# Four cross-attention layers on one core: the maximum's quarters and spread in the maximum's own PSUM banks, and grouped logits issued between the masked exponentials with their maxima held back

## The chip, the core and the metric

One NeuronCore of one Trainium2 chip runs the whole program. The metric is the device time of the core in microseconds; lower is better. Three runs of the kernel before gave 3663.92, 3665.89 and 3667.55 us, a median of 3665.89 us.

## What is computed

Four attention layers, one after the other, on four batch entries of 512 positions by 256 channels, all in 32-bit floats. Layers 0, 2 and 3 are "masked": 16 heads of 64, keys and values from a context of 1024 positions by 512 channels, with a bias of -20 on a few context positions where a mask over query positions is 0. Layer 1 is "grouped": an RMS norm, 16 query heads of 16 and 4 key and value heads.

```python
# layers 0, 2, 3 (T = 1024 keys, HW = 512 queries, HEAD_DIM = 64)
q = hidden_states @ Wq
k = encoder_hidden_states @ Wk
v = encoder_hidden_states @ Wv
...
logits = jnp.einsum('bhqd,bhkd->bhqk', q, k) * scale
logits = logits + col_bias[None, None, :, :]
probs = jax.nn.softmax(logits, axis=-1)
out = jnp.einsum('bhqk,bhkd->bhqd', probs, v)
out = out.transpose(0, 2, 1, 3).reshape(B, HW, HEADS * HEAD_DIM)
out = out @ Wo + bo
out = out + residual
# layer 1
xn = rmsnorm(x, norm_w)
...
scores = jnp.einsum('btgrd,bsgd->bgrts', qg, k) * scale
attn = jax.nn.softmax(scores.astype(jnp.float32), axis=-1).astype(q.dtype)
out = jnp.einsum('bgrts,bsgd->btgrd', attn, v).reshape(B, T, N_HEADS * HEAD_DIM)
return residual + out @ wo
```

## The kernel before

**Units and steps.** A unit is two heads of one layer of one batch entry: 96 masked units (three layers, four entries, eight units) and 32 grouped ones. Two strings, `MASKED_TURNS` and `GROUPED_TURNS`, give 96 steps; each step has one masked unit `g`, and 32 of them, from the 13th to the 74th, also have a grouped unit `lam`. Within a batch entry the grouped units come in every second step, and the last two in neighbouring steps. At the step before its own, a grouped unit is called `coming`: there its logits are made. The masked unit of the step before is `g1`.

**Tiles.** A unit's logits are held transposed, keys on partitions: eight tiles `g.st[t]` of 128 x 1024 (128 keys, two heads of 512 queries). TensorE makes a tile in two PSUM banks, ScalarE copies it to SBUF, and VectorE keeps a running maximum over the tiles in the two banks of tile 0, `g.mx_place`. `max_quarters` (line 759) reduces this maximum over partitions: a reduction with 32 x 32 transposes into one bank (L755), then small copies and maxima (L765 to L770). `max_everywhere` (line 775) spreads the result over all partitions with a transpose (L781), for a masked unit into two further banks, for a grouped one into SBUF. Then the tiles are lowered by it (L789 on VectorE for masked, L787 on GpSimd for grouped units) and ScalarE takes the exponential in place (L795). GpSimd adds a masked unit's exponentials up (L834). `attend` (L734) multiplies by the values one step later for a masked unit, and in the same step for `lam`. `normalise` (VectorE, L755 to L880) turns the sums into reciprocals, through one scratch bank, and scales the output; `project_out` (L898) adds it to the state.

**PSUM.** There are eight banks. The class `Place` gives out one bank, or an even-odd pair, when an instruction is issued; `back` returns it and numbers the return. A pair is the one whose later return is oldest; a single bank is the one with the oldest return, where 2 is added if the other half of its pair is free too. The place is a matter of issue order only: on the chip, the next user of a bank waits until the last one has read it.

**The order.** Every engine runs its instructions in the order in which the program issues them; that order is written out by hand. A step issues, in turn: for `lam`, the eight subtractions on GpSimd; the scores of `g` (L704, L710; copies L714, maxima L718); a single bank for the output of `g1` (`place_out`); the first four exponentials of `lam`; the maximum of `g`; `attend(g1)`. Then comes a list `fill` of TensorE work with estimated durations: the output projections, the query projections (L622, copy L628), and in odd steps the keys of the next two masked units (four halves of two parts, L526, copy L531), in even steps their values (L565, copy L572). Keys, values and queries each take a single bank, which is returned when the copy is issued. A clock `now` adds up the estimates. Three kinds of work are put in by due time:

- the subtractions and exponentials of `g` and the rest of `lam`'s exponentials are `events`; `pass_events(now)` issues those that are due just before the copy of a fill item;
- `pairs`: each of four pairs of logits tiles of `coming` (`logits_pair`, L681, copies L687, maxima L693), from 13.0 in steps of 2.5 (12.0 if there is a `lam`). Before the first pair, `behind_exponentials` issues all events that are left, and what was put off in `late`: `normalise(g1)` and the end of `lam`'s output. After the fourth pair come `max_quarters` and `max_everywhere` for `coming`;
- `attend_grouped`, the attention of `lam`, is put into `fill` once 9.5 of work stand before it (and after all projections of grouped outputs).

DMA loads for later steps are issued at the end of a step on SyncE.

Of the kernel before, what the change touches and what calls it, by code (L numbers as in the profile page):

```python
# [12 lines left out]
ALU = mybir.AluOpType  # L13
# [7 lines left out]
NT = T // P  # L21
# [61 lines left out]
def kernel(ctx: ExitStack, tc: tile.TileContext, a: dict, out: bass.AP):  # L83
    nc = tc.nc
# [8 lines left out]
    def t_(shape, tag, name, bufs=1, dtype=FP):  # L93
        return sb.tile(shape, dtype, tag=tag, name=name, bufs=bufs)
# [4 lines left out]
    ps_all = ps.tile([P, 8, S], FP, tag="ps", name="ps")  # L99
    given_back = dict.fromkeys(range(8), 0)  # L100
    returns = [0]

    class Place:
        def __init__(self, width=2):
            free = given_back
            if width == 2:
                at = min(
                    (n for n in range(0, 8, 2) if n in free and n + 1 in free),
                    key=lambda n: max(free[n], free[n + 1]),
                )  # L110
            else:
                at = min(free, key=lambda n: free[n] + (2 if n ^ 1 in free else 0))
            self.banks = range(at, at + width)
            for n in self.banks:
                del free[n]
            self.ap = ps_all[:, at : at + width, :].rearrange("p n q -> p (n q)")
# [13 lines left out]
    def take_set(g):  # L130
        g.set = sets_free.pop(sets_free.index(min(sets_free)))
        g.st = [st_slot((NT + 1) * g.set + t) for t in range(NT)]
        g.mx = st_slot((NT + 1) * g.set + NT)

    def give_set(g):
        sets_free.append(g.set)
# [539 lines left out]
    def logits_pair(g, i):  # L676
        ws = [Place(), Place()]
        for odd in range(2):
            for j in range(2):
                rows = slice(64 * odd + 32 * j, 64 * odd + 32 * (j + 1))  # L680
                nc.tensor.matmul(  # L681
                    ws[odd].ap[:, j * S : (j + 1) * S], lhsT=g.kt[rows, i * P : (i + 1) * P],
                    rhs=g.qt[rows, :], start=True, stop=True,
                )
        for odd, w in enumerate(ws):
            t = 2 * i + odd
            nc.scalar.copy(g.st[t], w.ap)  # L687
            if t == 0:
                g.mx_place = w
            else:  # L690
                w.back()
                top = g.mx_place.ap
                nc.vector.tensor_tensor(top, top, g.st[t], ALU.max)  # L693

    def scores(g):
        take_set(g)
# [23 lines left out]
    def place_out(g, width=1):  # L720
        g.place = Place(width)
        g.po, g.psum = g.place.ap[:, 0:S], g.place.ap[:, S:]

    def attend(g, blocks=range(NT)):
        for t in blocks:
            for j in range(2):
                rows = g.rows[j]
                if not g.masked:
                    rows = slice(64 * g.h + 32 * j, 64 * g.h + 32 * (j + 1))
                at, first, last = rows, 0, NT - 1  # L730
                if not g.masked:
                    at = slice(64 * (t % 2) + 32 * j, 64 * (t % 2) + 32 * (j + 1))
                    first, last = t % 2, NT - 2 + t % 2
                nc.tensor.matmul(  # L734
                    g.po[at, :], lhsT=g.v[:, t, rows], rhs=g.st[t][:, j * S : (j + 1) * S],
                    start=(t == first), stop=(t == last),
                )

    def keep_even(g):


        if g.h == 0:
            gq[g.b, "o"] = t_([P, S], "o1", f"o1_{g.name}")
        nc.scalar.copy(gq[g.b, "o"][64 * g.h : 64 * (g.h + 1), :], g.po[0:64, :])

    def keep_odd(g):
        half = gq[g.b, "o"][64 * g.h : 64 * (g.h + 1), :]
        nc.vector.tensor_tensor(half, half, g.po[64:128, :], ALU.add)  # L748
        g.place.back()
# [4 lines left out]
    def over_quarter(out_, of, op):  # L754
        nc.vector.tensor_reduce(  # L755
            out_, of.rearrange("p (b x) -> p b x", x=32), AX.X, op, apply_transpose=True
        )

    def max_quarters(g):
        w = Place(1)  # L760
        quarter, half = w.ap[:, 0:32], w.ap[0:64, 32:64]
        other = t_([64, 32], "other_max", f"other_max_{g.name}")
        over_quarter(quarter, g.mx_place.ap, ALU.max)
        g.mx_place.back()
        nc.vector.tensor_copy(other, quarter[64:128, :])  # L765
        nc.vector.tensor_tensor(half, quarter[0:64, :], other, ALU.max)
        nc.vector.tensor_copy(other[0:32, :], half[32:64, :])
        g.every = t_([P, 2 * S // 32, 1], "every", f"every_{g.name}")
        for h in range(4):
            nc.vector.tensor_tensor(  # L770
                g.every[32 * h : 32 * (h + 1), :, 0], half[0:32, :], other[0:32, :], ALU.max
            )
        w.back()

    def max_everywhere(g):
        if g.masked:
            g.mb_place = Place()
            g.mb = g.mb_place.ap
        else:
            g.mb = g.mx  # L780
        nc.vector.transpose(  # L781
            g.mb.rearrange("p (b r) -> p b r", r=32), g.every.to_broadcast([P, 2 * S // 32, 32])
        )

    def subtract(g, t):
        if not g.masked:
            nc.gpsimd.tensor_tensor(g.st[t], g.st[t], g.mb, ALU.subtract)  # L787
            return
        nc.vector.tensor_tensor(g.st[t], g.st[t], g.mb, ALU.subtract)  # L789
        if t == NT - 1:  # L790
            g.mb_place.back()

    def exponentials(g, t):
        st = g.st[t]
# [41 lines left out]
    def turn_grouped(g):  # L836
        w = Place(1)
        normalise_grouped(g, w.ap)
        w.back()
# [118 lines left out]
    def at(n):  # L958
        return steps[n] if 0 <= n < len(steps) else (None, None)
# [8 lines left out]
    def head(g):  # L968
        return steps[step_of[1, g.b, 0]][1]

    def share(g):

        g.kt = head(g).kts[g.h]
        if g.h == 1:
            g.qt = steps[step_of[1, g.b, g.u - 1]][1].qts[1]
# [53 lines left out]
    for n in range(len(steps) + 2):  # L1029
        g, lam = at(n)  # L1030
        follows, coming = at(n + 1)
# [55 lines left out]
        ready = []  # L1087
        events = []
        late = []
        pairs = []  # L1090

        def pass_events(us):
            while events and events[0][0] < us:
                events.pop(0)[2]()

        def behind_exponentials():
            pass_events(99.0)
            while late:
                late.pop(0)()

        def pair(i):
            if i == 0:
                behind_exponentials()
                take_set(coming)
            logits_pair(coming, i)
            if i == NT // 2 - 1:
                max_quarters(coming)
                max_everywhere(coming)

        if coming:  # L1110
            share(coming)
        queries = []
# [18 lines left out]
        if g:  # L1131
            max_quarters(g)
            max_everywhere(g)
# [19 lines left out]
                    events.append((2.3 * t - 7.0, lam, lambda t=t: exponentials(lam, t)))  # L1153
            events.sort(key=lambda e: e[0])
        if coming:
            pairs += [((12.0 if lam else 13.0) + 2.5 * i, i) for i in range(NT // 2)]

# [2 lines left out]
        fill, of_grouped = (  # L1162
            [
                (1.8 * len(each), lambda each=each: project_out(*each))
                for each in outs if each[0].masked == m
            ]
            for m in (True, False)
        )
# [9 lines left out]
        if lam:  # L1178

            def attend_grouped():  # L1180
                while any(of is lam for _, of, _ in events):
                    events.pop(0)[2]()
                lam.v = head(lam).v
                place_out(lam)
                attend(lam)
                give_set(lam)
                late.append(lambda: keep_odd(lam))
                if lam.h == 1:
                    late.append(lambda: turn_grouped(lam))
                return lambda: keep_even(lam)  # L1190

            total, where = 0.0, 0
            first_at = max((fill.index(each) + 1 for each in of_grouped), default=0)
            while where < len(fill) and (total < 9.5 or where < first_at):
                total += fill[where][0]
                where += 1
            fill.insert(where, (3.6, attend_grouped))
# [26 lines left out]
        now = 0.0  # L1224
        for us, w in fill:
            while pairs and pairs[0][0] <= now:
                pair(pairs.pop(0)[1])
                now += 1.0
                pairs = [(max(at, now + 1.6), i) for at, i in pairs]
            done = w()  # L1230
            now += us
            if callable(done):
                pass_events(now)
                done()
        while pairs:
            pair(pairs.pop(0)[1])
        behind_exponentials()
        ready += turned
# [38 lines left out]
```

## Time and profile before

| | |
|---|---|
| median of three runs | 3665.89 us |
| the profiled execution | 3666.02 us |
| its span, first to last instruction | 3664.2 us |
| TensorE busy | 3550.1 us |
| VectorE busy | 3019.4 us |
| ScalarE busy | 2317.6 us |
| GpSimd busy | 2219.7 us |
| granted TensorE clock, mean | 0.998 |
| span from 34.24 to 398.76 us (eleven steps without a grouped unit) | TensorE busy 364.02 of 364.52 us |
| 398.76 to 2951.33 us (the 63 steps around the grouped units) | 2460.75 of 2552.57 us |
| 2951.33 to 3664.20 us (the rest) | 703.27 of 712.87 us |

Busy time is the time in which at least one instruction of the engine runs. A matmul's end is modelled, and matmuls overlap: a 32-bit matmul of 128 x 512 stands in the trace as two records of about 0.6 us that start 0.43 us apart. So the spacing of starts, and not the duration of one, tells what TensorE does in a time. A row of the timeline merges neighbouring instructions of one kind; in brackets behind it stands the idle time of the engine before it and what ended it. In the sum of waits a row reads: who waited, for whom, total us, how often, the longest.

### The profile page before, as it was taken

The numbers are of one execution on the slowest core, as the hardware profiler recorded it, in microseconds if no ns is written. First come the engines' busy times: TensorE is split into PE (matmuls) and PEld (weight loads), VectorE is DVE, ScalarE is ACT, GpSimd is POOL, SyncE is SP. The second block draws the span as 40 slices with busy tenths as digits, with TensorE's granted clock in tenths as the row PEclk, the third lists the DMA queues.
The fourth block names the chain that finished last, engine by engine and source line by source line (L and its number), as shares of the span: only waits on it lengthen the run. The fifth ranks groups of instructions, "written<-read, shape, count | busy, mean of one in ns | idle before, by whom it ended". The sixth has DMA issues, their size and how long they took to land.

```text
span 3664.2 us, 40591 instructions
## 1 busy us (share of the span) xinstructions
PE 3550.1 (97%) x14510; PEld 1719.1 (47%) x14510; DVE 3019.4 (82%) x4134; ACT 2317.6 (63%) x2657; POOL 2219.7 (61%) x1005
## 2 busy tenths in 40 slices
PE   8999999999999999999999999999999999999998
PEld 4554444444454444444444444444444445454454
DVE  7877788888878878897888889788878978888787
ACT  4556566666756666675666667566666765555554
POOL 3565466656746665684666658556765755545454
PEclk9999999999999999999999999999999999999999
DMA  3231101101021011102101110110002011002100
GB/s 88 61 118 53 55 28 41 31 18 51 19 67 42 26 30 48 57 19 61 49 26 28 55 51 19 53 56 27 28 28 72 19 32 49 18 26 72 32 29 8
DMA packets 164845, 154.69 MB, mean 42 GB/s; under 512 B 42776, under 2 KB 142616, under 8 KB 164132
## 3 DMA queue, kind: packets, MB, share of 16 engines
q1 hardware_dynamic: 158990, 139.00, 12.1%
q0 software_dynamic: 2560, 8.39, 0.7%
q10 hardware_dynamic: 3094, 4.72, 0.6%
q8 instruction: 114, 1.87, 0.2%
q14 instruction: 87, 0.71, 0.1%
HBM read 133.20 MB, written 14.68 MB: 40 GB/s over the span
## 4 chain that ended last, share of the span: by engine, by line
PE 76%; DVE 15%; ACT 6%; issue 2%; ACTq 0%; DMA 0%; DVEq 0%; POOL 0%; POOLq 0%
PE ps L734 16%; PE ps L526 16%; PE ps L565 15%; PE ps L704 15%; PE ps L898 4%; PE ps L622 4%; PE ps L681 4%; DVE ps L718 4%; DVE st L789 3%; ACT st L795 3%; DVE ps L755 2%; DVE ps L693 2%; ACT st L714 2%; ACT st L687 1%; DVE ps L781 1%
## 5 line engine op out<-in xcount | busy, mean ns | idle before, releaser
L834 POOL TENSOR_TENSOR st<-st 128x1024 f32<-128x1024 f32 x668 | 1579.6, 2365 | 1112.6 <-ACT st L795 1067.7
L795 ACT ACTIVATE st<-st 128x1024 f32<-128x1024 f32 x1024 | 1038.3, 1056 | 570.2 <-DVE st L789 499.6
L718 DVE TENSOR_TENSOR ps<-ps,st 128x1024 f32<-128x1024 f32 x672 | 827.6, 1232 | 384.0 <-ACT st L714 323.3
L789 DVE TENSOR_TENSOR st<-st,ps 128x1024 f32<-128x1024 f32 x768 | 881.2, 1215 | 3.3
L734 PE MATMUL ps<-st,v 128*64 128x512 f32 (+1 forms) x4064 | 802.1, 596 | 8.5 <-ACT st L795 8.5
L704 PE MATMUL ps<-qt,kt 64*128 64x512 f32 x3072 | 732.8, 604 | 75.4 <-DVE ps L755 45.2
L714 ACT COPY st<-ps 128x1024 f32<-128x1024 f32 x768 | 718.8, 1044 | 128.4 <-PE ps L710 64.3
L787 POOL TENSOR_TENSOR st<-st 128x1024 f32<-128x1024 f32 x256 | 596.8, 2376 | 295.3 <-DVE st L781 295.3
L526 PE MATMUL ps<-ctx,wk 128*128 128x512 f32 x1536 | 692.4, 600 | 2.2 <-ACT ctx L428 2.2
L565 PE MATMUL ps<-wv,ctx 128*128 128x256 f32 x3072 | 682.3, 381 | 0.0
L565 PEld LDWEIGHTS ps<-wv,ctx 128*128 128x128 f32 x3072 | 581.5, 190 | 130.6 <-issue 53.5
L704 PEld LDWEIGHTS ps<-qt,kt 64*128 64x128 f32 x3072 | 315.6, 187 | 434.9 <-issue 130.3
L734 PEld LDWEIGHTS ps<-st,v 128*64 128x64 f32 (+1 forms) x4064 | 242.2, 130 | 545.0 <-issue 432.3
L526 PEld LDWEIGHTS ps<-ctx,wk 128*128 128x128 f32 x1536 | 285.7, 191 | 394.0 <-issue 369.4
L693 DVE TENSOR_TENSOR ps<-ps,st 128x1024 f32<-128x1024 f32 x224 | 276.1, 1232 | 86.8 <-ACT st L687 75.4
L687 ACT COPY st<-ps 128x1024 f32<-128x1024 f32 x256 | 247.0, 1015 | 87.0 <-PE ps L681 86.6
L572 ACT COPY v<-ps 128x512 f32<-128x512 f32 x192 | 110.5, 576 | 150.9 <-PE ps L565 150.6
L628 ACT ACTIVATE qt<-ps 128x512 f32<-128x512 f32 x96 | 56.6, 590 | 220.2 <-PE ps L622 220.2
L622 PE MATMUL ps<-x,wq 128*128 128x512 f32 x384 | 188.1, 613 | 1.1 <-ACT x L391 1.1
L681 PE MATMUL ps<-qt,kt 32*128 32x512 f32 x1024 | 171.5, 640 | 8.0 <-DVE o L748 5.2
L898 PE MATMUL ps<-ot,wo 128*128 128x512 f32 x384 | 177.9, 606 | 0.7 <-DVE ot L880 0.7
L531 ACT COPY kt<-ps 128x512 f32<-128x512 f32 x192 | 110.8, 577 | 101.5 <-PE ps L526 97.2
(142 smaller groups left out, 1696.4 us busy)
## 6 DMA issues: line engine op xcount, KB each, us to landing
ctx<-kept SPq DMA_DIRECT2D x30, 1024.0 KB, 8.0
wk<-in_L_xattn_Wk_dram SPq DMA_DIRECT2D x47, 512.0 KB, 3.6
wv<-in_L_xattn_Wv_dram SPq DMA_DIRECT2D x47, 512.0 KB, 3.7
wq<-in_L_xattn_Wq_dram SPq DMA_DIRECT2D x96, 128.0 KB, 3.5
wo<-in_L_xattn_Wo_dram SPq DMA_DIRECT2D x96, 128.0 KB, 3.9
st<-kept SPq DMA_DIRECT2D x4, 2048.0 KB
kept<-st SPq DMA_DIRECT2D x12, 512.0 KB, 3.2
qt<-qt ACTq DMA_DIRECT2D x32, 128.0 KB, 2.2
```

What stands on the lines that cost most here:

```text
L526: nc.tensor.matmul(m, lhsT=g.w["k"][:, k, :], rhs=ctx_half[g.b, n][:, k, :], start=(k == 0), stop=(k == KT - 1),)
L565: nc.tensor.matmul(m[:, half * 2 * P : (half + 1) * 2 * P], lhsT=ctx_half[g.b, t // 4][:, k, t % 4 * P : (t % 4 + 1) * P], rhs=g.w["v2"][: ...
L622: nc.tensor.matmul(m, lhsT=g.wq[:, k, :], rhs=x[:, k, :], start=(k == 0), stop=(k == KC - 1))
L693: nc.vector.tensor_tensor(top, top, g.st[t], ALU.max)
L704: nc.tensor.matmul(m[:, j * S : (j + 1) * S], lhsT=g.kt[g.rows[j], keys], rhs=g.qt[g.rows[j], :], start=True, stop=t > 0,)
L714: nc.scalar.copy(g.st[t], m)
L718: nc.vector.tensor_tensor(top, top, g.st[t], ALU.max)
L734: nc.tensor.matmul(g.po[at, :], lhsT=g.v[:, t, rows], rhs=g.st[t][:, j * S : (j + 1) * S], start=(t == first), stop=(t == last),)
L787: nc.gpsimd.tensor_tensor(g.st[t], g.st[t], g.mb, ALU.subtract)
L789: nc.vector.tensor_tensor(g.st[t], g.st[t], g.mb, ALU.subtract)
L795: nc.scalar.activation(st, st, AF.Exp)
L834: nc.gpsimd.tensor_tensor(g.acc, g.st[0] if t == 1 else g.acc, g.st[t], ALU.add)
```

## The change

- `max_quarters` takes no bank of its own: the quarters and the halves go into the first columns of the running maximum's banks. A grouped unit's pair is returned after the last of the small operations (before: after the quarters).
- `max_everywhere` spreads a masked unit's maximum into the same pair, which is returned after the eighth subtraction.
- In a step with a `coming` unit, a single bank whose partner is free carries a penalty of 99 in place of 2.
- `logits_pair` no longer issues the running maxima; they gather in `tops` and are issued by `catch_up`, when no events are left after a fill item, or with the fourth pair. `catch_up` issues the remaining events and `late` first.
- The first pair no longer issues everything left (unless there is a `lam`), and pairs are due from 9.5 instead of 13.0 in steps without a `lam`; due events are issued before each pair.
- `attend_grouped` is put behind 13.0 of work instead of 9.5 in steps without a `coming` unit.

```diff
+    apart = [2]
...
-                at = min(free, key=lambda n: free[n] + (2 if n ^ 1 in free else 0))
+                at = min(free, key=lambda n: free[n] + (apart[0] if n ^ 1 in free else 0))
...
             else:
                 w.back()
-                top = g.mx_place.ap
-                nc.vector.tensor_tensor(top, top, g.st[t], ALU.max)
+
+    def maximum(g, t):
+        top = g.mx_place.ap
+        nc.vector.tensor_tensor(top, top, g.st[t], ALU.max)
...
     def max_quarters(g):
-        w = Place(1)
-        quarter, half = w.ap[:, 0:32], w.ap[0:64, 32:64]
+        top = g.mx_place.ap
+        quarter, half = top[:, 0:32], top[0:64, 32:64]
         other = t_([64, 32], "other_max", f"other_max_{g.name}")
-        over_quarter(quarter, g.mx_place.ap, ALU.max)
-        g.mx_place.back()
+        over_quarter(quarter, top, ALU.max)
...
-        w.back()
+        if not g.masked:
+            g.mx_place.back()
 
     def max_everywhere(g):
         if g.masked:
-            g.mb_place = Place()
-            g.mb = g.mb_place.ap
+            g.mb = g.mx_place.ap
...
         if t == NT - 1:
-            g.mb_place.back()
+            g.mx_place.back()
...
-        pairs = []
+        pairs, tops = [], []
...
+        def catch_up():
+            behind_exponentials()
+            while tops:
+                maximum(coming, tops.pop(0))
+
         def pair(i):
             if i == 0:
-                behind_exponentials()
+                if lam:
+                    behind_exponentials()
                 take_set(coming)
             logits_pair(coming, i)
+            tops.extend(range(max(2 * i, 1), 2 * i + 2))
             if i == NT // 2 - 1:
+                catch_up()
                 max_quarters(coming)
                 max_everywhere(coming)
 
+        apart[0] = 99 if coming else 2
...
-            pairs += [((12.0 if lam else 13.0) + 2.5 * i, i) for i in range(NT // 2)]
+            pairs += [((12.0 if lam else 9.5) + 2.5 * i, i) for i in range(NT // 2)]
...
-            while where < len(fill) and (total < 9.5 or where < first_at):
+            while where < len(fill) and (total < (9.5 if coming else 13.0) or where < first_at):
...
             while pairs and pairs[0][0] <= now:
+                pass_events(now)
                 pair(pairs.pop(0)[1])
...
+            if tops and not events:
+                catch_up()
         while pairs:
+            pass_events(now)
             pair(pairs.pop(0)[1])
```

## The prediction, made before the changed kernel was run

> **What bounds the kernel now.** I read the page first, then the sum of waits, then the timeline around one step.
>
> ```profile
> PE 3550.1 (97%) x14510; PEld 1719.1 (47%) x14510; DVE 3019.4 (82%) x4134; ACT 2317.6 (63%) x2657; POOL 2219.7 (61%) x1005
> PEclk9999999999999999999999999999999999999999
> ```
> TensorE is busy for 97% of the span. Its idle time is 3664.2 - 3550.1 = 114.1 us, and no change that leaves the matmuls as they are can save more than that. The sum of waits says where most of it lies:
>
> ```profile
> PE ps L704 <- DVE ps L755: 45.2, 28, 2.1
> PE ps L704 <- ACT st L687: 27.4, 24, 1.2
> PE ps L734 <- ACT st L795: 8.5, 10, 1.2
> PE ps L681 <- DVE o L748: 5.2, 4, 1.3
> ```
> Together 86.3 us, all in steps with a grouped unit. I call a step that makes the coming unit's logits (and uses none) a making step (28, four of them a batch's first), one that uses a unit and makes none a using step (28), and four do both; 36 have none. The first two rows are one pattern at the end of 24 making steps: scores tile 0 waits for the copies of the last logits pair (1.14 us), tile 2 for the max of quarters (1.70). A typical making step (queues interleaved in the timeline, one row per run of instructions; start, duration, engine):
>
> ```profile
> 1466.10 3.48 DVE L789 TENSOR_TENSOR st<-st,ps 128x1024 f32<-128x1024 f32 x3
> 1466.69 1.88 PE L622 MATMUL ps<-x,wq 128*128 128x512 f32 x4
> 1468.41 8.75 PE L526 MATMUL ps<-ctx,wk 128*128 128x512 f32 x20
> 1469.45 0.58 ACT L628 ACTIVATE qt<-ps 128x512 f32<-128x512 f32 x1
> 1471.88 2.19 ACT L795 ACTIVATE st<-st 128x1024 f32<-128x1024 f32 x2 [0.91 <-DVE st L789]
> 1473.98 0.57 ACT L531 COPY kt<-ps 128x512 f32<-128x512 f32 x1
> 1474.44 3.02 ACT L795 ACTIVATE st<-st 128x1024 f32<-128x1024 f32 x3
> 1476.29 1.25 DVE L755 TRANSPOSE_TENSOR_REDUCE ps<-st 128x32 f32<-128x1024 f32 x1
> 1477.37 0.57 ACT L531 COPY kt<-ps 128x512 f32<-128x512 f32 x1
> 1478.25 0.69 DVE L864 TENSOR_TENSOR short<-ps,other 32x16 f32<-32x16 f32 x4
> 1478.32 1.93 ACT L687 COPY st<-ps 128x1024 f32<-128x1024 f32 x2 [0.38 <-PE ps L681]
> 1480.95 1.14 PE L681 MATMUL ps<-qt,kt 32*128 32x512 f32 x8
> 1489.42 1.13 PE L704 MATMUL ps<-qt,kt 64*128 64x512 f32 x4 [1.14 <-ACT st L687]
> 1493.32 6.02 PE L704 MATMUL ps<-qt,kt 64*128 64x512 f32 x24 [1.70 <-DVE ps L755]
> ```
> To be seen here: TensorE runs from the query (L622) through 20 key matmul records (L526) without a gap, although ScalarE copies the query out only at 1469.45 to 1470.03 and the first keys at 1473.98, some 1.5 us and 2 us after TensorE finished them. Those copies wait behind exponentials, which wait for VectorE's subtractions. TensorE doesn't notice, because each result is in another bank.
>
> **The change part by part.** The profile prints no bank numbers, so I follow the allocator's rule by hand.
>
> *In-place maximum* (all steps): no instruction more or less; the quarters still read 1024 columns (1265 ns from PSUM, 1253 from SBUF) and the spread still writes 1024. Bound from both sides: L718, which reads and writes the same PSUM banks, takes 1232 ns, L789, which reads PSUM and writes SBUF, 1215, so 17 ns either way on 224 instructions, 4 us of VectorE. I take 0: in the 36 steps without a grouped unit TensorE covers it (idle 0.5 us between 34.24 and 398.76), and in the others VectorE is busy 33.81 of 40.56 us. Without that cover it costs those 4 us.
>
> *The 99.* In a making step, a single bank is taken beside an occupied one, or else a pair is broken. The output of the previous masked unit (`place_out(g1)`) takes half of a pair, X0, before the fill begins, and keeps it until `normalise(g1)` has been issued. All other pairs are whole or wholly taken, so X1 is the only bank without the penalty. The banks' counts differ by some tens of returns at most, under 99. So query, first keys, second keys and the scratch bank of `normalise` all take X1, one after the other. Before, a penalty of 2 let them go round. That is a new chain of waits, TensorE behind ScalarE, and I walk it with the rows above. A key half is 8 records at 429 ns spacing, 3.43 us, a part half of that.
>
> 1. Query ends 1468.57; its copy, in unchanged ScalarE order, ends 1470.03. First keys start 1470.1 and not 1468.41.
> 2. They finish issuing at 1473.5 and end at 1473.7. Their copy stands behind exponential 4 (1471.88 + 2.19 = 1474.07) and ends 1474.64. Second keys start 1474.7, 2.9 us later than 1468.41 + 3.43.
> 3. By due times pair 0 now comes after 3.6 + 1.7 + 3 x 1.7 = 10.4, between the parts of the second keys: TensorE 1476.5 to 1477.6, second part ends 1479.4. ScalarE: exponential 5, two logits copies (1.93) from 1477.7, exponentials 6 and 7 (2 x 1.01), then the keys' copy: 1477.7 + 1.93 + 2.02 + 0.57 = 1482.2.
> 4. The events are now used up, so `catch_up` issues `normalise`. Its quarters write X1 and wait for that copy. From L755's start to L864's end is 1478.94 - 1476.29 = 2.65 us, so X1 is free at 1482.3 + 2.65 = 1484.95. After it the four pairs' counts make X1 the oldest, and the third keys take it: they start at 1485.0. Pair 1 covers TensorE only until 1480.7, so it idles 4.3 us.
> 5. From there part 1.91 (with the switch of shape), pair 1.08, part 1.91, pair 1.08, parts 1.72 + 1.76: next scores at 1494.5, against 1489.42. **+5.1 us** although the 1.14 before tile 0 is gone.
> 6. VectorE: `normalise` ends 4.41 after 1482.3, at 1486.7; seven maxima of 1.28 to 1495.7; quarters and small ones 2.72 to 1498.4. Tile 2 still falls on the maximum's pair, now given back after the small ones, and is due at 1496.4: a wait of 2.1, about what was there.
>
> Queued behind the waiting TensorE are pairs 2 and 3, the last keys and the next scores, so nothing hides it. 24 x 5.1 = 122.
>
> *Batch-first making steps* (4): two queries share X1. The second starts at 1069.8 (copy L628 ends 1069.71) and not 1067.84, the keys after its two copies (1074.41) and not at 1069.55, 4.9 late; with the wait of point 4 (3.3 here, since pair 2 fills some) less what the values afterwards absorb I take 7.5 each, 5 to 8.5. 30 us.
>
> *Steps that do both* (4): their waits, 1.31 and 1.01, may go (-2.3), or X1 costs as above (+5.1). Their value copies are also late (first at 1434.86 in a using step, its matmuls done by 1433), but `normalise` is issued before pair 0 as it was. I take +2: 8 us.
>
> *Attention behind two more parts* (using steps): the row of 8.5 us goes, since the exponentials gain 3.4 us. Bounds -8.5 and 0 (if the later sum makes another wait); I take -8.5. The added SP and POOL work is none: loads are issued at the step's end as before.
>
> *Logits earlier, maxima held back*: counted in points 3 to 6. By itself it swaps order only; TensorE has no gap there to fill.
>
> Sum: 122 + 30 + 8 - 8.5 = 152. The profiled execution took 3666.0 (span 3664.2 and 1.8 around it), 0.1 above the median of the three runs. 3666 + 152 = **3818 us**.
>
> *The clock.* A wait of 4.3 us is longer than any in the middle of this trace, and there the clock is touched already:
>
> ```profile
> 2710.00:2715.00 5.00, 5.00 (x17) 2.27 (x15) 4.65 (x10) 2.26 (x3) 2.48 (x2) 0.66 0.00 0
> ```
> In this stretch, just after an idle of 2.05 us, the granted clock (third number from the end) was 0.66: 0.34 x 5 = 1.7 us lost. 1820 to 1825 shows 0.84, 2139 to 2144 0.68; the other boundaries, with the same wait, nothing. Bounds for 28 long waits: 0 and 28 x 1.7 = 48 us. I take 0, since TensorE would be 2.1 us early at tile 2 and can lose 1.7 on the way; without that cover it is 48.
>
> [...]
>
> **The rivals.**
> - *The boundary waits go and the shared bank is hidden*: **faster**. For it: 86.3 us of waits that the change aims at. Against: point 1 needs only two rows of this trace. It decides from where the new waits of a making step stay under the 1.14 + 1.70 removed. At best 3666 - 86 = 3580. 10%.
> - *`normalise` finds another bank*, so only the ScalarE waits count: 5.1 - 4.3 = 0.8 a step. 24 x 0.8 + 4 x 5 + 8 - 8.5 = +39: 3705. Against it: the penalty leaves only X1. 8%.
> - *Gains and waits cancel, and the reordering does nothing*: 3666. For it: the copies' order barely changes. 4%, mostly within 0.2%.
> - *The clock drops at every long wait*: 3818 + 48 = 3866. For it the 0.66; against it the cover at tile 2. 8%.
>
> **How the numbers follow.** The forecast (3770 to 3850) has 70%. The range 3690 to 3866 takes in the second rival and the clock's bound and leaves out about 18%. A measurement tells 0.2%, 7 us, from no change. Faster 0.10, within 0.03, slower 0.87.
>
> **What would show it.** Key matmuls L526 waiting for ACT L628 and L531 and for DVE L864 (before: 2.2 us of idle in all); a TensorE gap near 4 us in each making step, behind pair 1; L681's wait pattern at the boundary gone, L704 behind the maximum's small ones still some 2 us; L734 behind L795 gone; making steps about 45 us and not 40.1. Wrong if L526 never waits: then the banks go round, or the copies come earlier than this walk has them.

## The result and the profile after

The changed kernel takes 3841.24 us (median of four runs, 3840.1 to 3846.25); the kernel before, run beside it, 3666.72. The ratio is 1.0479, with a 95% interval of 1.0461 to 1.0497: slower by 174.5 us. The forecast was 3818, in a range of 3690 to 3866. The profiled execution took 3840.10 us over a span of 3838.3, 174.1 more than before.

The first line of the page after, and its row for the key matmuls (L527 now, their copy L532; the last part of a row is the idle time before the group and what ended most of it), with the row of the kernel before behind it:

```profile
PE 3595.5 (94%) x14510; PEld 1699.1 (44%) x14510; DVE 3023.0 (79%) x4134; ACT 2306.3 (60%) x2657; POOL 2218.7 (58%) x1005
...
L527 PE MATMUL ps<-ctx,wk 128*128 128x512 f32 x1536 | 753.3, 636 | 157.8 <-DVE short L866 75.5
...
L526 PE MATMUL ps<-ctx,wk 128*128 128x512 f32 x1536 | 692.4, 600 | 2.2 <-ACT ctx L428 2.2
```

The same 14510 matmul records are there. TensorE's idle time has grown from 114 to 3838.3 - 3595.5 = 243 us, and the group that never waited before (2.2 us) now has 158 us of it. The mean of a key matmul went from 600 to 636 ns too, although its size is the same. The sum of waits names what it waits for:

```profile
DVE ps L758 <- ACT kt L532: 199.2, 28, 11.0
PE ps L527 <- DVE short L866: 75.5, 23, 4.1
PE ps L707 <- DVE every L772: 42.3, 28, 4.7
PE ps L527 <- ACT kt L532: 31.3, 24, 2.7
PE ps L527 <- issue: 20.3, 5, 4.1
PE ps L527 <- ACT qt L629: 17.6, 18, 1.0
```

Rows two, four and six are the chain of the one shared bank: keys behind the query's copy (L629), behind the first keys' copy (L532), behind the last reader of the scratch (L866). Row five belongs to the scratch too, as one of its waits below shows. With row two that makes 28 waits behind the scratch: 18 of about 4.1 us and ten of 2.2. The first row is the link between: the quarters of the sums (L758) wait in each of 28 steps until ScalarE has copied the second keys out. The third row is score tile 2 at the boundary, still there; the one of tile 0 is gone. One making step of the kind walked in the prediction, from the timeline:

```profile
1536.11 1.88 PE L623 MATMUL ps<-x,wq 128*128 128x512 f32 x4
...
1538.36 0.58 ACT L629 ACTIVATE qt<-ps 128x512 f32<-128x512 f32 x1
...
1538.99 3.70 PE L527 MATMUL ps<-ctx,wk 128*128 128x512 f32 x8 [1.00 <-ACT qt L629]
...
1543.50 1.98 PE L527 MATMUL ps<-ctx,wk 128*128 128x512 f32 x4 [0.81 <-ACT kt L532]
...
1550.36 0.59 ACT L532 COPY kt<-ps 128x512 f32<-128x512 f32 x1
...
1551.05 1.26 DVE L758 TRANSPOSE_TENSOR_REDUCE ps<-st 128x32 f32<-128x1024 f32 x1 [5.77 <-ACT kt L532]
...
1553.01 0.70 DVE L866 TENSOR_TENSOR short<-ps,other 32x16 f32<-32x16 f32 x4
...
1553.81 3.63 PE L527 MATMUL ps<-ctx,wk 128*128 128x512 f32 x4 [4.06 <-issue]
1568.03 5.42 PE L707 MATMUL ps<-qt,kt 64*128 64x512 f32 x24 [0.55 <-DVE every L772]
```

The third keys start at 1553.81, a tenth of a microsecond after L866 ended (1553.01 + 0.70), and 4.06 us after the matmuls before them. "issue" stands there, but the semaphore wait of L527 in the queue of the weight loads lasted 5.13 us, from 1548.63 to 1553.76, and the end of L866 shows for what. Then comes what the forecast had priced at nothing: these four records take 3.63 us, where the same four took 1.98 in 1543.50. The windows show why (the last but two is the granted clock):

```profile
1550.00:1555.00 5.00, 1.19 (x2) 0.70 (x3) 3.67 (x11) 2.77 (x4) 4.84 (x3) 0.88 0.00 2
1555.00:1560.00 5.00, 5.00 (x16) 1.46 (x14) 4.43 (x5) 1.40 (x2) 1.01 (x3) 0.78 0.19 26
```

In the clock records of this trace the granted clock is 0.50 for one stretch of 3.41 us, from 1553.78, where the wait ends. The whole run has 49 such stretches before the program's end (some two in a row), 167 us, against 3 and 10 us in the kernel before.

Six of the 24 making steps, from 1175.61, 1603.32, 1868.68, 2296.24, 2564.76 and 2992.54 us, have another order. There the next masked unit is the first of a layer, and its query (L623) stands last but one in the list and not ahead of the keys. From the first of them, rows of TensorE and VectorE:

```profile
1215.83 9.11 DVE L696 TENSOR_TENSOR ps<-ps,st 128x1024 f32<-128x1024 f32 x7
...
1217.25 1.99 PE L623 MATMUL ps<-x,wq 128*128 128x512 f32 x4
...
1227.75 7.97 PE L707 MATMUL ps<-qt,kt 64*128 64x512 f32 x24 [4.67 <-DVE every L772]
```

TensorE waits 2.6 to 2.7 us for the first keys' copy and 2.2 behind the scratch in these six, and in four of them tile 2 of the next scores then waits 4.67 us for the held-back maxima (L696). In the 18 others that wait is 0.55 to 0.73 us.

Where the time went by kind of step (a step runs from its first bias matmul, line 710 or 713, to the next one's; us over all steps of the kind, in brackets the part at half clock; the program's last step is left out):

| kind of step | before | after | change | forecast |
|---|---|---|---|---|
| 35 without a grouped unit | 1155.8 | 1155.3 | -0.5 | 0 |
| 24 making | 963.9 | 1133.3 (122.9) | +169.4 | +122 |
| 4 making, first of a batch | 201.1 | 229.6 (13.7) | +28.5 | +30 |
| 4 that do both | 178.2 | 184.3 (6.8) | +6.1 | +8 |
| 28 using | 1086.0 (10.2) | 1056.6 (23.9) | -29.4 | -8.5 |

### The profile page after: what moved, and what is told of

It is laid out like the page before. It is cut to its first block, busy times and chain, and to the rows that moved or that the text cites. A ratio compares the mean times of both kernels' runs of the same rounds, so it can differ in the third digit from the quotient of the medians.

```text
span 3838.3 us, 40377 instructions
## 1 busy us (share of the span) xinstructions
PE 3595.5 (94%) x14510; PEld 1699.1 (44%) x14510; DVE 3023.0 (79%) x4134; ACT 2306.3 (60%) x2657; POOL 2218.7 (58%) x1005
## 4 chain that ended last, share of the span: by engine, by line
PE 70%; DVE 21%; ACT 6%; issue 2%; DMA 0%; DVEq 0%; POOL 0%; ACTq 0%; POOLq 0%
PE ps L566 17%; PE ps L737 15%; PE ps L527 13%; PE ps L707 12%; DVE ps L721 6%; DVE st L791 4%; PE ps L623 4%; PE ps L682 3%; DVE ps L696 3%; DVE ps L758 3%; PE ps L900 2%; ACT st L688 2%; ACT st L797 1%; ACT st L717 1%; DVE every L772 1%
## 5 line engine op out<-in xcount | busy, mean ns | idle before, releaser
L527 PE MATMUL ps<-ctx,wk 128*128 128x512 f32 x1536 | 753.3, 636 | 157.8 <-DVE short L866 75.5
L791 DVE TENSOR_TENSOR st<-st,ps 128x1024 f32<-128x1024 f32 x768 | 881.2, 1215 | 3.3
L737 PE MATMUL ps<-st,v 128*64 128x512 f32 (+1 forms) x4064 | 789.8, 596 | 0.0
L707 PE MATMUL ps<-qt,kt 64*128 64x512 f32 x3072 | 722.5, 607 | 52.1 <-DVE every L772 42.3
L527 PEld LDWEIGHTS ps<-ctx,wk 128*128 128x128 f32 x1536 | 293.8, 200 | 597.8 <-issue 418.3
L707 PEld LDWEIGHTS ps<-qt,kt 64*128 64x128 f32 x3072 | 287.6, 189 | 427.7 <-issue 174.5
L696 DVE TENSOR_TENSOR ps<-ps,st 128x1024 f32<-128x1024 f32 x224 | 275.9, 1232 | 47.8 <-ACT st L688 33.3
L758 DVE TRANSPOSE_TENSOR_REDUCE ps<-st 128x32 f32<-128x1024 f32 x93 | 116.7, 1255 | 216.1 <-ACT kt L532 199.2
L532 ACT COPY kt<-ps 128x512 f32<-128x512 f32 x192 | 111.5, 581 | 159.1 <-PE ps L527 158.8
L629 ACT ACTIVATE qt<-ps 128x512 f32<-128x512 f32 x96 | 56.6, 590 | 242.1 <-PE ps L623 242.1
L623 PE MATMUL ps<-x,wq 128*128 128x512 f32 x384 | 188.1, 613 | 1.1 <-ACT x L392 1.1
```

The costliest lines, as they stand in the source:

```text
L527: nc.tensor.matmul(m, lhsT=g.w["k"][:, k, :], rhs=ctx_half[g.b, n][:, k, :], start=(k == 0), stop=(k == KT - 1),)
L623: nc.tensor.matmul(m, lhsT=g.wq[:, k, :], rhs=x[:, k, :], start=(k == 0), stop=(k == KC - 1))
L707: nc.tensor.matmul(m[:, j * S : (j + 1) * S], lhsT=g.kt[g.rows[j], keys], rhs=g.qt[g.rows[j], :], start=True, stop=t > 0,)
L737: nc.tensor.matmul(g.po[at, :], lhsT=g.v[:, t, rows], rhs=g.st[t][:, j * S : (j + 1) * S], start=(t == first), stop=(t == last),)
```

## The experiments

Each ratio is to the kernel before, run on the same chip. Diffs are against the changed kernel unless the text says otherwise.

### Scratch bank taken by age again

```diff
     def normalise(g):
+        kept, apart[0] = apart[0], 2
         w = Place(1)
+        apart[0] = kept
```

> The changed kernel, but the scratch bank of normalise is the one with the oldest return again (penalty 2 for this one bank). Theory, the bank chain: the wait of the third keys behind VectorE's small sums (4.06 us in the making step from 1519 us) goes, the two waits behind ScalarE's copies (1.0 and 0.8) stay. 24 x 4.06 = 97 us, and the granted clock, which falls after that wait, comes back near 0.995, worth 20 to 30 more: 3841 - 97 - 25 = about 3720 us. Rival, the copies alone hold TensorE back: the third keys then wait for the copy of the second keys anyway (it ended at 1550.95, the keys started at 1553.81, so 2.9 of 4.06 would go): 3841 - 70 = about 3770 us or more, clock still near 0.98.

3744.04 us, ratio 1.0212 (1.0195 to 1.0229): 97 us less than the changed kernel, between the two expectations. The largest wait of the keys in this kernel:

```profile
PE ps L527 <- ACT kt L532: 53.5, 42, 2.7
```

The waits of the keys behind L866 are gone. But the row behind the copies rose from 31.3 us in 24 waits to 53.5 in 42: in the 18 making steps with the long wait, the third keys still use the bank of the second and wait 1.24 us for their copy. So the 4.06 us were two parts, some 1.2 for ScalarE's copy and 2.8 for VectorE's small sums, in 18 steps and not in 24. The half clock fell from 167 to 72 us, and the granted clock over the span is 0.990 where the changed kernel had 0.978.

### Normalise ahead of the first logits pair

```diff
                 if lam:
                     behind_exponentials()
+                while late:
+                    late.pop(0)()
                 take_set(coming)
```

> The changed kernel, but normalise of the unit before is issued ahead of the first logits pair, so that its output bank is free and its scratch is taken before the single banks are crowded. Theory, the bank chain: third keys wait no more, only the query's and the first keys' copies (1.0 + 0.8 a making step) are left: 3841 - 24 x 4.06 - 25 for the clock - 10 in the four batch-first steps = about 3705 us. Rival, the earlier logits themselves (between the exponentials, in front of copies that the next matmuls need) hold TensorE back: their order on ScalarE is the same here, so the time stays above 3780 us.

3717.98 us, ratio 1.0137 (1.012 to 1.0154): 123 us less, near the theory's 3705 and far from the rival. ScalarE's order is the changed kernel's here, with logits between the exponentials. What is left:

```profile
PE ps L527 <- ACT kt L532: 31.3, 24, 2.7
PE ps L682 <- DVE ot L882: 22.1, 10, 2.2
PE ps L527 <- ACT qt L629: 17.7, 18, 1.0
```

The two copy waits are untouched, the scratch wait is gone. A new row (L682 behind L882) is the first pair, which now waits for a bank of the output just scaled, 2.2 us in each of ten steps: the six with the late query and the four batch-first ones.

### Query and first keys go round

```diff
-        apart[0] = 99 if coming else 2
+        apart[0] = 99 if coming and lam else 2
...
+            if coming and now >= 8.0:
+                apart[0] = 99
             while pairs and pairs[0][0] <= now:
```

> The changed kernel, but the penalty of 99 begins only at 8.0 of the step's work, so that the query and the first keys go round over the banks, and second keys and scratch still share one. Theory, the bank chain: the waits of 1.0 and 0.8 us behind ScalarE's copies go; the second keys' copy still stands behind logits copies and exponentials, so the wait behind the scratch stays or grows, up to the 1.8 saved. Saved 24 x 0 to 1.8 and some 4 us in each batch-first step: 3841 - 16 - 0 to 43 = 3780 to 3825 us, clock still near 0.98. Rival, the two copies start the delay and all later waits follow from it: the scratch wait shrinks too, under 3760 us.

3795.36 us, ratio 1.0348 (1.033 to 1.0365): 46 us less, in the favourable half of the theory's span. The wait behind the scratch:

```profile
PE ps L527 <- DVE short L866: 73.4, 23, 3.9
```

Both rows behind L629 and L532 are gone and the scratch wait is as long as ever (73.4 us, 75.5 before the edit). So it does not follow from the two early waits; they add up. The half clock even rose, to 198 us (granted clock 0.973).

### Eight matmuls in the idle stretch

```diff
         def catch_up():
+            cold.extend(late)
             behind_exponentials()
...
             tops.extend(range(max(2 * i, 1), 2 * i + 2))
+            if cold and not lam:
+                cold.clear()
+                for _ in range(8):
+                    nc.tensor.matmul(
+                        last_pair[0][:, 0:S], lhsT=aug_k[0], rhs=aug_q, start=True, stop=True
+                    )
```

> The changed kernel with eight bf16 matmuls of 128x512 added to each of 28 steps (1.7 us of TensorE work each, into a bank whose logits are copied already, result unused), between the pair after normalise and the third keys, where TensorE waits. They add work and take no wait away. Theory, the clock: the idle stretch falls from 4 us to about 2, the clock is halved less often (167 us of the changed kernel's profile at half clock before, under 80 now), and what it costs shows: 3841 - 15 to - 40 = 3800 to 3825 us in spite of the added work. Rival, the half clock costs nothing because TensorE would wait for VectorE at the third score tile anyway: 3841 us within 5, or more where the added matmuls push the keys back.

3829.52 us, ratio 1.0442 (1.0425 to 1.046): 12 us less than the changed kernel, with 28 x 1.9 us of matmuls added, a little short of what the theory asked and outside the rival's 5. The half clock fell from 167 to 116 us only, where under 80 was expected (granted clock 0.984; 10 of the 116 lie at the program's start, where the changed kernel's profile has none). The 24 making steps took 1105.5 us, 27.8 less (half clock there 54.6 and not 122.9), but the using steps 7.4 more. The waits show what they gave back:

```profile
PE ps L710 <- DVE every L775: 57.2, 28, 4.7
```

The row is score tile 2 (L710 in this kernel): 57.2 us and not 42.3. The added matmuls themselves wait 42.8 us in all for the copy of the bank that they write. What TensorE gained by a full clock it partly waited for VectorE at the boundary, so that cover was real and incomplete. The four steps that do both, where nothing was added, took 10.8 us more with 13.7 us more at half clock: in three of them tile 2 now waits 4.73 us, and two stretches follow; in the changed kernel one of the four had such a wait (4.66).

### Both remedies together

The edits of the second and the third experiment in one kernel (normalise first; query and first keys go round):

```diff
+                while late:
+                    late.pop(0)()
...
-        apart[0] = 99 if coming else 2
+        apart[0] = 99 if coming and lam else 2
...
+            if coming and now >= 8.0:
+                apart[0] = 99
```

> The changed kernel with both remedies: normalise ahead of the first logits pair, and the penalty of 99 only from 8.0 of the step's work on. All else of the change stays: in-place maximum, logits from 9.5, maxima held back, attention at 13.0. Theory, the loss is all in the shared bank: with no matmul behind a copy or a small sum that is late, the time falls to about that of before, 3650 to 3690 us, and the clock to 0.995 or more. Rival, earlier logits or held-back maxima cost something by themselves: it stays above 3700 us, with the waits elsewhere.

3671.39 us, ratio 1.0013 (1.0004 to 1.0022), as the theory had it: with the waits on the shared bank gone, 170 of the 174 us are gone. The clock came to 0.992 and not to the 0.995 expected; 58 us are still at half clock, 10 of them at the program's start. One of the two edits moves VectorE's work too, and not only the choice of a bank; the two that touch the choice alone (the first and the third experiment) brought 97 and 46 us, and no run joins them. What is left of the change costs about what its moved attention brings (25 us, next experiment), so, as an estimate, in-place maximum, early logits and held-back maxima still cost some 29 us together. The largest wait of TensorE in this kernel:

```profile
PE ps L682 <- DVE st L791: 34.9, 28, 1.8
```

The logits now wait for the subtraction to leave the masked maximum's banks (L791), the price of keeping the spread there with the logits drawn forward.

### The attention's place alone

Against the kernel before:

```diff
-            while where < len(fill) and (total < 9.5 or where < first_at):
+            while where < len(fill) and (total < (9.5 if coming else 13.0) or where < first_at):
```

> The kernel before with one part of the change alone: the grouped attention behind 13.0 of work in place of 9.5 in the 28 steps that only use a grouped unit. Theory of the prediction: only the ten waits of TensorE behind exponentials go, 8.5 us: 3658 us. The using steps of the changed kernel, 29 us shorter in sum, suggest more: up to 29 us, 3638 us, if that gain belongs to this part; if it stays at 3658, the rest of the 29 came from waits moved into the steps before.

3642.43 us, ratio 0.9928 (0.9915 to 0.9942): 25 us less, three times the 8.5. In the timeline of the kernel before, a grouped attention takes two rows, from 1516.83 to 1522.33, 5.50 us; in this kernel one of 3.64:

```profile
1516.83 3.63 PE L734 MATMUL ps<-st,v 128*32 128x512 f32 x28
...
1521.28 1.05 PE L734 MATMUL ps<-st,v 128*32 128x512 f32 x4 [0.82 <-ACT st L795]
```

```profile
1513.99 3.64 PE L734 MATMUL ps<-st,v 128*32 128x512 f32 x32
```

Only 0.82 of the 1.86 us saved stood as idle time of TensorE. The rest was in waits shorter than the modelled ends of the matmuls in flight, which count as busy. The weight loads' row shows them: this sum of waits has 14.7 us there, the kernel before 40.7, a difference of 26.

```profile
PEld ps L734 <- ACT st L795: 40.7, 78, 2.1
```

```profile
PEld ps L734 <- ACT st L795: 14.7, 47, 0.8
```

### The in-place maximum alone

Against the kernel before, nothing but these places:

```diff
-        w = Place(1)
-        quarter, half = w.ap[:, 0:32], w.ap[0:64, 32:64]
+        top = g.mx_place.ap
+        quarter, half = top[:, 0:32], top[0:64, 32:64]
...
-        g.mx_place.back()
...
-        w.back()
+        if not g.masked:
+            g.mx_place.back()
...
-            g.mb_place = Place()
-            g.mb = g.mb_place.ap
+            g.mb = g.mx_place.ap
...
-            g.mb_place.back()
+            g.mx_place.back()
```

> The kernel before with the in-place maximum alone: quarters and spread in the maximum's own banks, nothing else. Prediction: no time in the 36 steps without a grouped unit. At the 24 boundaries the grouped maximum's pair is returned after the small operations and not after the quarters, 1.4 us later (from the end of L755 to the end of L770), but it also moves in the order of pairs; so between 0 and 24 x 1.4 = 34 us more, 3667 to 3700. Rival, it helps by the bank it frees: under 3660.

3689.76 us, ratio 1.0061 (1.0047 to 1.0075): 22 us more, within the span expected, and no help from the bank it frees.

```profile
PE ps L709 <- DVE every L774: 89.1, 28, 3.3
```

Before, tile 0 and tile 2 waited 27.4 + 45.2 = 72.6 us at the boundaries; now one wait of 3.2 us on the mean in each of 28 steps makes 89.1, since the pair comes back after the last small operation. In the 35 steps without a grouped unit the sum is 1156.6 us against 1155.8. The half clock is 79 us against 10 (granted clock 0.989 and 0.998): a stretch follows 16 of the 24 waits of 3.33 us.

### A faster kernel

The changed kernel with the maximum's own banks as before, the penalty left at 2, and pairs due from 11.0:

```diff
-        apart[0] = 99 if coming else 2
+        apart[0] = 2
...
-            pairs += [((12.0 if lam else 9.5) + 2.5 * i, i) for i in range(NT // 2)]
+            pairs += [((12.0 if lam else 11.0) + 2.5 * i, i) for i in range(NT // 2)]
```

> A search for the better kernel: of the change, the held-back maxima and the earlier logits (from 11.0 and not 9.5) and the attention at 13.0, but the maximum's quarters and spread in banks of their own and the penalty left at 2, so that single banks go round. Theory: the wait of score tile 0 (27 us over 24 steps) goes because key parts stand behind the last pair, the attention's waits go, the one of tile 2 stays: 3667 - 27 - 8 to - 29 = 3611 to 3632 us at best. Rival, with two broken pairs the logits wait for banks and the gain is lost: 3660 us or more.

3622.42 us, ratio 0.9875 (0.986 to 0.989): 45 us less than the kernel before, in the middle of the theory. The held-back maxima and the earlier logits do what they can do: the wait of tile 0 is gone, and tile 2's fell from 45.2 to 27.8 us. Half clock is 20 us (granted clock 0.997), 10 of them at the program's start.

```profile
PE ps L707 <- DVE ps L758: 27.8, 28, 1.4
```

## Why the prediction was right, and which terms were mis-sized

**The sign and the mechanism** were right and are shown: the penalty of 99 sends query, keys and scratch through one bank, and TensorE runs behind ScalarE's and VectorE's reading of it. Taking the scratch alone out of that bank brings 97 us, taking query and first keys out 46, and with the waits on the bank gone 170 of 174 us are gone (3671). In the step shown, the waits behind copies came out shorter than walked: the keys started 1.16 and 1.08 us late (idle 1.00 and 0.81) against 1.7 and 1.2, and VectorE began the quarters of that step 0.43 us earlier in it, without the 0.47 us that it idled before; the wait behind the scratch was 4.06 against 4.3.

**The making step's 5.1** was right for the order that was walked, which 18 of the 24 steps have. The kernel with the added matmuls shows it without the clock: they fill the wait, and its third keys start at the same place in the step. The step shown above, in the changed kernel and then in that one (the last but two is the granted clock):

```profile
1519.23:1566.23 47.00, 41.13 (x144) 15.27 (x142) 36.38 (x44) 25.60 (x29) 19.42 (x11) 0.96 0.20 65
1510.27:1555.58 45.31, 41.33 (x154) 15.51 (x151) 35.30 (x43) 25.61 (x29) 19.39 (x11) 1.00 0.21 67
```

In the kernel before the step took 40.56 us, so at full clock it is 4.75 longer. Eight of the 18 steps have the full clock in the kernel with the added matmuls, and are 4.7 to 5.1 longer than before; tile 2 then waits about 1.7 us, where 2.1 had been walked.

**The six steps with the late query were the largest error.** The walk took one order for all 24, and 5.1 for each. As an estimate, take each making step together with the step after it, less what the attention alone brings there: the 18 cost 5.6 us each, 101 in all, the six 10.1 each, 60 in all. The forecast had 94 for the 18 and 37 for the six (24 x 5.1, and 2 for each of the four that a step that does both follows). The 4.67 us at tile 2 was not foreseen, nor that it brings the half clock with it.

**The clock, taken as 0,** fell in 23 of the 24 making steps. The cover named in the prediction, that TensorE would be early at tile 2, was there in part: in the step shown that wait shrank to 0.55 us, and tile 2 began at 1568.03 us, where the walk, moved to this step, has 1567.8 (1498.4 and 69.4 us later). This step and the one after it took 84.08 us, and 83.52 in the kernel with the added matmuls, so one stretch cost 0.56 us and not 1.7. Eleven of the 18 steps have two stretches, and the four of them that have none in the other kernel show 1.7 for both. As an estimate 7 x 0.56 + 11 x 1.7 = 23 us for the 18, where the prediction kept 48 for 28 waits as its bound. In the six steps no run parts the clock from the waits.

**The attention's 8.5** should have been 25 by itself. It was read from TensorE's idle row, where the weight loads' row was the one that showed the wait.

**The in-place maximum's 0** holds only in the steps without a grouped unit. By itself it costs 22 us at the boundaries. Inside the change the walk had the later return (point 6), and no run shows its share there.

For batch-first steps (30 against 28.5) and steps that do both (8 against 6.1) the sums were near, partly by luck. The first kind waits 2.2 us behind the scratch and not the 3.3 taken, but has 13.7 us at half clock; of the four that do both, three changed by less than 1 us and one grew by 6.0, with 4.66 us of wait at tile 2 and two stretches of half clock. And 152 came near 174 because errors have opposite signs: the six steps too low by some 24 and the 18 by some 8, the attention's gain too low by 12 to 16.

**The rivals.** A hidden shared bank didn't happen. Another bank for the scratch, priced at 3705, took 3744 when it was made: the copy's wait behind it had been left out, and the clock. The half clock at every long wait, put at 8%, did come: a stretch began during each of the 22 waits of 4.06 us and more, or up to 0.27 us after it. But it did not cost the 48 us of that rival, since part of it was covered, and the 3841 lies between forecast and rival.

## What to carry to other kernels

A rule that packs buffers to keep large places free must be walked for what it does in time: the same free space may hang one engine on another's reading of a single buffer. Walk every order in which a step occurs: six of 24 steps differed from the one walked and cost twice as much. Price a new long TensorE wait with the clock, not only with its length (here the half clock came with each of the 22 waits of 4.06 us and more), and ask what covers it. And read the weight loads' waits beside TensorE's idle time, since short waits can vanish under the modelled ends of matmuls: moving the attention took 26 us out of the first, where the second had shown 8.5.

## What the runs showed of the hardware

In the traces of the changed kernel and of the kernel before, the granted clock is 0.50 in stretches of 3.41 us, one or two at a time (49 and 3 ahead of the program's end), and in each of the two traces these stretches begin whole multiples of 3.4133 us apart. In the changed kernel one begins during each of the 22 TensorE waits of 4.06 us and more, or up to 0.27 us after it. In the kernel before they follow 3 of the 24 boundaries, by 1.2 to 1.7 us, where waits of 1.1 and 1.7 to 2.05 us stand close together; the 3.41 us ahead of these stretches hold 1.70 to 2.05 us of idle time. What a stretch cost differed with what covered it: 0.56 us in the step shown, and among the six steps with the late query 1.7 for one stretch (46.2 us against 44.5) and 2.75 for two (47.2).
